# The seams of a three-stage sequence kernel: the first norm of its last block and its stores moved into the streams, keys and first maxima merged with the groups before them, and four heads scored at once where no maxima are due

## The chip, the cores and the metric

The kernel runs on one core of one Trainium2 chip. The metric is the time of one execution on the device in microseconds (us), and lower is better. Data are float32, with a few masks and index vectors in bfloat16.

Engines: PE does matmuls (PEld is its load of weights, which overlaps), DVE vector operations, ACT activations and copies, POOL further vector operations, and SP issues most DMAs. Each engine takes its own queue in order. PE writes into PSUM, which here is eight banks of 128 partitions x 512 floats; DVE and ACT read the results from there.

## The reference, cut to what matters

One sequence `x` of 2048 tokens with 128 features passes through four residual blocks:

```python
x = x + L0_attn(layernorm(x))   # LinOSS state space model, gated
x = x + L0_ffn(layernorm(x))    # 8 experts, top 1: relu(h @ We[e] + be[e]) * p
x = x + L1_attn(layernorm(x))   # causal attention, 16 heads of 8, softmax
x = x + L1_ffn(layernorm(x))    # 6 layers, each: local attention (16 heads of 64,
                                # windows of 32, rotary), then a gated feed-forward
```

The state space model is a recurrence along time, `z1 = m11 z + m12 y + f1 bu`, `y1 = m21 z + m22 y + f2 bu`, with two components (real and imaginary) for each of 128 states; then `o = ys[0] @ C0.T - ys[1] @ C1.T + x * D`, normed, multiplied by a gate `g * sigmoid(g)` and projected. The causal attention needs, for each query and head, the maximum of its scores (or any value that keeps the exponentials in range), the exponentials, their sum and the weighted values. The last block is itself a small network whose input is `layernorm(x)`; its output is added to `x`.

## The kernel before

**Grid.** 2048 tokens are 16 tiles of 128 (NT), and 4 groups (NG) of 4 tiles, each group 512 tokens wide (GW). Almost every operation on PSUM is 128 x 512.

**Order of work.** The wrapper `InOrder` (line 59) keeps what it issues in program order on its engine, so the order in which the Python code calls `self.pe`, `self.dve` and so on is the order of the queues. The trace names the wrapper's line, 66, for all of these; they are told apart by the names of their tiles. `interleave` (line 71) merges generators: each job yields how long to wait in a made-up time, and the one that is due first goes on.

**Stages 1 and 2 (`front`, line 458).** `ssm_inputs` (line 244) of each group, started 5.0 apart: layer norm (`norm_transposed`), `px` into `xsT`, two `pb` into `f1`, then `pg`, the gate. `ssm_scan` (line 277) then runs on DVE: 16 steps inside chunks of 16 tokens, a doubling scan over the 128 chunks, and 16 steps that give `yo`, one operation for each component. POOL meanwhile forms the powers (`ssm_powers`) after it has finished the gates. Then a second `interleave` (line 513) merges, for each group, `ssm_out`, `experts` and `keys_values`. An expert group holds two banks, `pi` and `py`, while DVE makes eight masked copies `own` (8 buffers) and PE multiplies each with its expert's matrix. `keys_values` makes the normed input `hT3`, the values `va`, and the keys `kT` for four groups of four heads. The PSUM pool of this part has 8 banks.

**Stage 3 (`stages123`, line 521).** The causal attention, for 16 blocks: 4 groups of heads times 4 groups of queries. Two streams of units:

- `maxima` (line 570): for one tile of queries and up to 512 keys, scores of two heads, then of the other two (`part`), then DVE's `reduce_max` (`rest`). When a block's maxima are done, `finish` subtracts them from the queries (`qT`), and only then may the block's attention begin.
- `attend` (line 627): for one tile of keys, scores of two heads at a time, `exp` on ACT, POOL's causal mask on the diagonal, and `pieces`, the weighing of the values (`av` on PE), put off by two half units.

Four heads' matmuls take 32 rows of the array each. The loop at line 758 runs ahead with the maxima: some units alone (the `while` at line 761), most paired with an attention unit (two heads of each at once), and where the maxima are far enough ahead an attention unit goes without them, still as two halves of two heads. `pass_unit` runs steps that were put off: `back`, `out_a`, `out_b`, which turn a finished block's result, project it, add `x` and write `x3T` (line 722). The pool of stage 3 has 7 banks under one tag and one for `av`.

**Stage 4 (`stage4`, line 807).** It first loads tables (`rot`, 1 MB, line 820) and masks, and norms `x3T` group by group into `s4[0]` (lines 853 to 861, with `norm_columns`, line 1192): mean by a matmul, difference, square, mean by a matmul, power on POOL, spread by a matmul, product. Then 96 tile steps (6 layers x 16 tiles) run as one software pipeline (`steps`, line 1172), in which `feed_forward` (line 1164) gives each step its parts of a group's feed-forward. Each tile also issues 14 to 16 small DMAs (`vw`) on SP. At the end `store` (line 1217) adds `x3T`, turns the result and stores it group by group: `yT`, `pst`, `ot`.

## Time and profile before

| | us |
|---|---|
| median of three runs (2693.87 to 2695.86) | 2695.79 |
| the profiled execution | 2700.82 |
| its span, first to last instruction | 2699.1 |
| SSM inputs, until the scan's first operation | 0 to 44.3 |
| scan on DVE, PE idle | 44.3 to 100.1 |
| SSM output, experts, keys and values | 100.1 to 207 |
| first maxima; first attention scores at 220.7 | 207 to 222 |
| attention, until the last `x3T` | 222 to 878 |
| first norm of stage 4, until its first projection | 878 to 909.5 |
| stage 4, with the stores at its end | 909.5 to 2699.1 |

Busy over the whole span: PE 2459.0 us (91%), DVE 1821.7 (67%), POOL 1658.8 (61%), ACT 1349.7 (50%). The mean granted clock of PE was 0.971.

How to read it: a timeline row gives start, duration, engine, line, operation, output and inputs, shapes, count, and, in brackets, the idle time of the engine before it with what ended it. A float32 matmul shows as two rows (`x2` for one). A row with a count covers that many instructions. A wait for several semaphores is put down to the last by the profile.

### The profile page before, as it was taken

To read this page: it belongs to the slowest core of one execution; us is meant where nothing else is said; L and a number is where in the kernel's file an instruction comes from. 1 tells how busy PE (TensorE), PEld (TensorE's weight loads), DVE (VectorE), ACT (ScalarE), POOL (GpSimd) and SP (SyncE) were. 2 spreads that over 40 slices of the span, in tenths; PEclk is the share of its full clock that TensorE was granted. 3 is DMA by queue.
4 is the path that set the end of the run, shared out by engine and by line. 5 is a ranking of instruction groups with operands and counts; after the bars stand their busy time and mean duration, and the time that the engine had idled before them with its cause. 6 is when DMAs were issued, how large, how long until landed. Compare 5 with 4: busy or idle time off the path is not lost.

```text
span 2699.1 us, 85362 instructions
## 1 busy us (share of the span) xinstructions
PE 2459.0 (91%) x37600; PEld 1478.4 (55%) x37600; DVE 1821.7 (67%) x2764; ACT 1349.7 (50%) x1806; POOL 1658.8 (61%) x1011
## 2 busy tenths in 40 slices
PE   3489999999999689999999999999999999999997
PEld 1473333333333366666666666666666666666664
DVE  6766664476642467777777777777777777777774
ACT  1132455544555144555555555555555555556552
POOL 4310000000001599989888888898888988898980
PEclk8689999999999799999999999999999999999999
DMA  2000000000000222233222322232323222222221
GB/s 82 1 1 1 1 1 1 2 1 1 1 1 1 62 65 69 60 88 72 59 66 67 89 58 71 66 87 60 73 62 82 69 66 67 59 60 65 60 59 43
DMA packets 93566, 128.39 MB, mean 48 GB/s; under 512 B 26248, under 2 KB 41104, under 8 KB 93072
## 3 DMA queue, kind: packets, MB, share of 16 engines
q1 hardware_dynamic: 92620, 122.48, 18.6%
q8 instruction: 299, 4.90, 0.8%
q10 hardware_dynamic: 580, 0.46, 0.1%
q14 instruction: 67, 0.55, 0.1%
HBM read 20.35 MB, written 1.05 MB: 8 GB/s over the span
## 4 chain that ended last, share of the span: by engine, by line
PE 63%; DVE 21%; ACT 6%; issue 5%; POOL 4%; SPq 1%; DMA 0%; DVEq 0%; ACTq 0%; POOLq 0%
PE sc L66 17%; PE ps L66 10%; PE av L66 6%; PE pt L66 5%; DVE mx L66 4%; PE py L66 4%; DVE rot_a L66 4%; DVE sm L66 4%; DVE ss L66 4%; PE ph L66 3%; DVE rot_b L66 3%; PE pto L66 3%; PE ptp L66 3%; ACT sq L66 3%; POOL sm L66 2%
## 5 line engine op out<-in xcount | busy, mean ns | idle before, releaser
L66 DVE TENSOR_REDUCE mx<-sc 128x1 f32<-128x512 f32 (+4 forms) x736 | 471.0, 685 | 238.9 <-PE sc L66 234.1
L66 POOL TENSOR_TENSOR rot_a<-rot_a,rot_b 128x1024 f32<-128x1024 f32 x192 | 459.2, 2392 | 144.1 <-DVE rot_b L66 143.9
L66 POOL TENSOR_TENSOR rn<-ss,mhalf 128x32 f32<-128x32 f32 x96 | 523.9, 5457 | 8.0
L66 ACT ACTIVATE ex<-sc 128x512 f32<-128x512 f32 (+3 forms) x640 | 310.0, 531 | 302.4 <-PE sc L66 301.3
L66 PE MATMUL sc<-kT,qT 64*32 64x64 f32 (+2 forms) x13568 | 429.7, 260 | 9.6 <-ACT qT L66 9.3
L66 POOL TENSOR_SCALAR_AFFINE_SELECT ex<-ex 128x512 f32<-128x512 f32 x64 | 40.6, 634 | 628.2 <-ACT ex L66 628.2
L66 DVE TENSOR_TENSOR rot_a<-ps,tab 128x1024 f32<-128x1024 f32 x192 | 235.0, 1224 | 221.9 <-ACT sq L66 205.3
L66 PE MATMUL sc<-qT,kT 32*128 32x512 f32 (+3 forms) x1280 | 369.4, 581 | 2.3 <-DVE qT L66 2.1
L66 PE MATMUL ps<-wqkv,s 128*128 128x512 f32 x768 | 367.8, 602 | 1.5 <-DVE rd L66 1.5
L66 ACT COPY vt<-pv 128x1024 f32<-128x1024 f32 x96 | 97.2, 1013 | 443.4 <-PE pv L66 425.4
L66 PEld LDWEIGHTS sc<-kT,qT 64*32 64x32 f32 (+1 forms) x13568 | 221.5, 113 | 139.1 <-issue 68.9
L66 ACT ACTIVATE sq<-ps 128x1024 f32<-128x1024 f32 x192 | 195.9, 1020 | 101.4 <-PE ps L66 101.4
L66 DVE TENSOR_REDUCE ss<-sq 128x16 f32<-128x1024 f32 x192 | 233.1, 1214 | 2.8
L66 DVE TENSOR_TENSOR rot_b<-ps,tab 128x1024 f32<-128x1024 f32 x192 | 233.0, 1213 | 0.0
L66 PEld LDWEIGHTS pt<-ident,rot_a 128*128 128x128 f32 x1536 | 175.5, 142 | 76.8 <-issue 40.3
L66 PEld LDWEIGHTS px<-oT,wo 128*128 128x128 f32 x1536 | 182.3, 193 | 63.5 <-ACT oT L66 61.4
L66 PEld LDWEIGHTS ps<-wqkv,s 128*128 128x128 f32 x768 | 138.6, 191 | 141.5 <-issue 136.7
L66 ACT ACTIVATE ex<-sm 128x1024 f32<-128x1024 f32 x96 | 101.5, 1057 | 221.2 <-POOL sm L66 221.2
L66 PE MATMUL pt<-ident,rot_a 128*128 128x128 f32 x1536 | 188.3, 275 | 23.3 <-POOL rot_a L66 23.1
L66 POOL TENSOR_TENSOR sm<-sm,rn 128x1024 f32<-128x1024 f32 x96 | 183.5, 1911 | 40.6 <-DVE rd L66 18.7
L66 DVE SCALAR_TENSOR_TENSOR act<-ph,vec,ge 128x512 f32<-128x512 f32 (+1 forms) x72 | 54.0, 750 | 220.1 <-ACT ge L66 220.0
L66 PE MATMUL px<-oT,wo 128*128 128x128 f32 x1536 | 194.9, 280 | 6.7 <-ACT oT L66 6.7
(212 smaller groups left out, 4014.2 us busy)
## 6 DMA issues: line engine op xcount, KB each, us to landing
vw<-vt SPq DMA_DIRECT2D x1524, 65.0 KB, 2.0
wqkv<-in_L_ffn_Wqkv SPq DMA_DIRECT2D x18, 512.0 KB, 5.1
wo<-in_L_ffn_Wo SPq DMA_DIRECT2D x6, 512.0 KB, 4.7
w<-in_L_ffn_W SPq DMA_DIRECT2D x6, 341.0 KB, 3.3
x<-in_L_attn_hidden_states SPq DMA_DIRECT2D x4, 256.0 KB, 4.3
rot<-in_rot SPq DMA_DIRECT2D x1, 1024.0 KB
out<-ot SPq DMA_DIRECT2D x4, 256.0 KB, 2.2
w<-in_L_ffn_W SPq DMA_DIRECT2D x12, 64.0 KB, 2.6
```

The lines of the kernel that those rows point to most:

```text
L66: return self._tc.keep_in_program_order(call(*args, **kw))
```

## The change

It has five parts, quoted below with lines left out where marked.

- `Merge` takes the place of `interleave`: jobs may be added while it runs, and it can stop when named jobs are done.
- SSM inputs: groups start 2.5 apart, the gate's projection waits 14.0 instead of 4.0; the two components of `yo` are written by one operation, into the memory of `f1`; the gate lies in the memory of `x3T`.
- `keys_values` makes the keys of the first head group alone; `keys` makes the others as a job of its own. The first maxima start as a job at 76, among the experts, and the attention is a job that is merged with what is left. The early part shares the 7 banks of the attention; `own` has 4 buffers.
- An attention unit without maxima scores all four heads, then weighs.
- The first norm of stage 4 is three put-off steps behind `out_b`; the stores are an eighth part of `feed_forward`, `yT` being formed in the last `ff_down` of a group. `rot` is loaded in two pieces.

```diff
+class Merge:
+    def __init__(self):
+        self.due, self.n, self.now = [], 0, 0.0
+    def add(self, wait, job):
+        heapq.heappush(self.due, (self.now + wait, self.n, job))
+        self.n += 1
+        return job
+    def run(self, jobs=None):
+        left = None if jobs is None else set(map(id, jobs))
+        while self.due and left != set():
+            self.now, _, job = heapq.heappop(self.due)
+            wait = next(job, None)
+            if wait is not None:
+                self.add(wait, job)
+            elif left is not None:
+                left.discard(id(job))
...
         self.dve.tensor_copy(xs_g, px)
-        yield 2.0
+        yield 3.0
...
-        yield 4.0
+        yield 14.0
         pg = psum.tile([P, G, P], F32, name="pg", tag="b")
...
-            for c in range(2):
-                dve.scalar_tensor_tensor(
-                    yo[c].rearrange("p (k l) -> p k l", l=CL)[:, :, l], cy[:, c], rows[:, 1, l : l + 1], t[:, c],
-                    ALU.mult, ALU.add,
-                )
+            dve.scalar_tensor_tensor(
+                yo.rearrange("p c (k l) -> p c k l", l=CL)[:, :, :, l], cy, rows[:, 1, l : l + 1], t,
+                ALU.mult, ALU.add,
+            )
...
-            own = pool.tile([P, GW], F32, name="own", bufs=EXPERTS)
+            own = pool.tile([P, GW], F32, name="own", bufs=4)
...
-        for grp in range(NGRP):
+        yield from self.keys(psum, g, hT3, kT, [0])
+
+    def keys(self, psum, g, hT3, kT, grps):
+        wqk, bqk, wv, wo, bo = self.w3
+        hg = hT3[:, g * GW : (g + 1) * GW]
+        for grp in grps:
             pk = psum.tile([P, GW], F32, name="pk", tag="b")
...
-            psum = ctx.enter_context(tc.tile_pool(name="s1p", bufs=8, space=PSUM))
...
-            begin = [(0, 9, 43), (9, 22, 58), (7, 40, 77), (18, 57, 82)]
...
+        begin = [(0, 9, 43, 51), (10, 22, 58, 66), (7, 41, 74, 87), (16, 57, 91, 111)]
+        wait = []
+        for g, (a, b, c, d) in enumerate(begin):
+            wait.append(merge.add(a, self.ssm_out(pool, psum, x, g, gate, xsT, yo)))
+            wait.append(merge.add(b, self.experts(pool, psum, x, g)))
+            merge.add(c, self.keys_values(kvpool, psum, x, g, hT3, kT, va))
+            merge.add(d, self.keys(psum, g, hT3, kT, range(1, NGRP)))
+        return wait
...
                     act.activation(xT[:, g * GW : (g + 1) * GW], po, AF.Identity, bias=bo)
+                    later(1, lambda: norm_a(g))
...
+            def norm_a(g):
+                xg = xT[:, g * GW : (g + 1) * GW]
+                pm = bank("pm")
+                pe.matmul(pm, lhsT=self.mean_w, rhs=xg, start=True, stop=True)
+                xc = pool.tile([P, GW], F32, name="nxc", tag="av", bufs=3)
+                dve.tensor_tensor(xc, xg, pm, ALU.subtract)
+                sq = pool.tile([P, GW], F32, name="nsq", tag="av", bufs=3)
+                act.activation(sq, xc, AF.Square)
+                later(1, lambda: norm_b(g, xc, sq))
+            def norm_b(g, xc, sq):
+                pvar = bank("pvar")[:, 0:G]
+                for j in range(G):
+                    pe.matmul(
+                        pvar[:, j : j + 1], lhsT=sq[:, j * P : (j + 1) * P], rhs=self.mean_w[:, 0:1],
+                        start=True, stop=True,
+                    )
...
+                self.rsqrt(r, var)
+                later(1, lambda: norm_c(g, xc, r))
+            def norm_c(g, xc, r):
+                pr = bank("prb")
...
+                    dve.tensor_tensor(
+                        self.s4_in[rs, g * GW + h : (g + 1) * GW + h], xc[rs], pr[rs], ALU.mult
+                    )
...
+            def catch_up(b, c):
+                nonlocal ahead
+                while ahead is not None and done - ahead[1] < wanted(b, c) - GW:
                     for rest in [step_m(ahead, pr) for pr in range(2)]:
                         rest()
                     pass_unit()
                     ahead = next_m()
-                while b not in found:
+                    yield 1.6
+            def weigh_due():
+                if pieces and pieces[0][0] <= halves:
+                    pieces.pop(0)[1]()
...
+                    if ahead is not None and done - ahead[1] < wanted(b, c_now):
+                        for half in range(2):
+                            rest = step_m(ahead, half)
+                            part(1 - half)
+                            weigh_due()
+                            if half:
+                                whole()
+                            rest()
+                            halves += 1
+                        pass_unit()
+                        ahead = next_m()
+                    else:
+                        for half in range(2):
+                            part(1 - half)
+                        weigh_due()
+                        halves += 1
+                        weigh_due()
+                        whole()
+                        halves += 1
+                        pass_unit()
+                    c_now += wd
+                    yield 3.3 * wd / GW
...
+            def begin():
+                nonlocal ahead
+                ahead = next_m()
+                yield 1.5
+                yield from catch_up(0, 0)
+            ahead = None
+            lead = merge.add(76.0, begin())
+            merge.run(wait)
+            early.close()
...
+            merge.run([lead])
+            merge.add(0.0, attention())
+            merge.run()
...
-            nc.sync.dma_start(rot, a["rot"])
+            for i0, i1 in ((0, 1), (1, NT)):
+                nc.sync.dma_start(rot[:, i0:i1], a["rot"][:, i0:i1])
...
-            for g in range(NG):
-                cols = slice(g * GW, (g + 1) * GW)
-                xc = pool.tile([P, GW], F32, name="xc")
-                pr = self.norm_columns(xc, x3T[:, cols], mean_w, pool, psum)
...
+                if g // NG == DEPTH - 1:
+                    yT = ff[g]["y"] = pool.tile([P, GW], F32, name="yT", tag="xc")
...
+                        dve.tensor_tensor(yT[rs], s4[0][rs, n + h : n + h + GW], x3T[rs, n : n + GW], ALU.add)
...
+            def store(g):
+                if g // NG == DEPTH - 1:
+                    yT = ff[g].pop("y")
+                    pt = big("pst")[:, 0].rearrange("p (j c) -> p j c", c=P)
+                    for j in range(G):
+                        pe.transpose(pt[:, j, :], yT[:, j * P : (j + 1) * P], self.ident)
+                    ot = pool.tile([P, G, P], F32, name="ot", tag="ff")
+                    dve.tensor_copy(ot, pt)
+                    sp.dma_start(o[:, g % NG * G : (g % NG + 1) * G, :], ot)
             parts = [
-                ff_mean, ff_var, ff_norm, lambda g: ff_up(g, 0), lambda g: ff_up(g, 1), lambda g: ff_up(g, 2), ff_down
+                ff_mean, ff_var, ff_norm, lambda g: ff_up(g, 0), lambda g: ff_up(g, 1), lambda g: ff_up(g, 2),
+                ff_down, store,
             ]
...
-            self.store(s4[0], x3T, out, pool, psum)
```

## The prediction, made before the result was known

> **What bounds the kernel now.** I read the table of 40 slices first, then the timeline at each place where PE falls off. In the slices (67.5 us each) PE is at nine tenths nearly everywhere; the exceptions are slices 1 to 3, slice 14 and the last, and in all but the last the granted clock falls as well.

> ```profile
> PE   3489999999999689999999999999999999999997
> ...
> DVE  6766664476642467777777777777777777777774
> ...
> PEclk8689999999999799999999999999999999999999
> ...
> PE 63%; DVE 21%; ACT 6%; issue 5%; POOL 4%; SPq 1%; DMA 0%; DVEq 0%; ACTq 0%; POOLq 0%
> ```

> The last line, the chain that ended last, says the same: PE 63%, with DVE as the second. So PE time counts wherever PE is full (the attention and stage 4), and waiting counts at the seams. The busy times of the stretches, from the query by windows (the columns after the length: PE, PEld, DVE, ACT, POOL, then clock, DMA share, GB/s), size the seams:

> ```profile
> 0.00:44.20 44.20, 25.34 (x72) 12.76 (x72) 18.85 (x68) 11.15 (x17) 7.27 (x13) 1.00 0.43 125
> 44.20:100.10 55.90, 0.00 (x0) 0.00 (x0) 52.91 (x123) 1.02 (x3) 39.76 (x93) 0.54 0.00 0
> ...
> 193.80:222.00 28.20, 21.55 (x111) 10.13 (x111) 14.56 (x40) 7.93 (x13) 3.92 (x6) 1.00 0.00 1
> 222.00:232.00 10.00, 10.00 (x45) 4.99 (x44) 5.53 (x15) 2.24 (x4) 0.64 (x1) 0.52 0.00 0
> ...
> 878.00:909.50 31.50, 19.79 (x73) 13.94 (x74) 7.74 (x17) 2.52 (x4) 6.46 (x17) 0.66 0.38 122
> ```

> The first is the SSM's inputs, with no engine full; the second the scan, which is DVE alone; the third the seam into the attention; the fourth the half clock behind it; the fifth the first norm of stage 4, one chain of waits per group.

> **Part a, the SSM inputs.** In the timeline the scan's first DVE operation starts at 44.28. DVE starts at 7.5 and owes each group 1.8 us of statistics (four pairs at 0.40, one 0.17), 1.1 of normalising, 0.69 for xsT and 1.07 for f1: 4.66, so 18.6 for four. The other 18 us it waits for PE (px 2.07 and pb 3.78 at low clock, 1.13 and 1.98 at full) in an order that lets a group's gate stand between. The change starts groups 2.5 apart, not 5, and moves the gates behind all f1. Following the new order with these durations, each DVE step waiting for the PE step before it, I get xsT of groups 0 and 1 at 16.5 and 21.6, then 5 us a group: f1 of group 3 ends at 36.7 (clock up early) to 38.5. I take **-6.5**; bounds -3 and -9. The gates (PE, ACT, POOL 1.27 each) go under the scan. POOL's powers are queued behind them: they ran from 47.3 to 71.6 and were needed at 82.7, so with the scan 6.5 earlier and the gates ending near 43 about 7 us of slack remain.

> **Part b, the scan.** Each of 16 steps now has one update of 128x256 where two of 128x128 stood (two in 0.54, start to start). Two independent 128x256 ones take 0.40 each (the zt pairs at 71.9 to 82.7), so 16 x 0.14 = **-2.2**.

> **Part c, keys and first maxima inside the early groups.** From 193.8 to 222 PE does 21.6 us of work; 6.6 us are idle: the last group's norm waits for the experts' sum, then pq for the keys, maxima for q, and DVE's last three reductions for the subtraction that frees the first scores. The next 10 us run at clock 0.52, a loss of 4.8. Within 100.1 to 193.8 PE is busy 83.2 of 93.7, another 10.5 of gaps. Nothing is removed; keys of groups 1 to 3 and the last two groups' values move into the attention's opening, where PE waits for maxima. Filled entirely, 6.6 + 4.8 + about half of 10.5 = 16.6. Against it: 4 own buffers where DVE ran 8 ahead (at 180.7, eight in 4.86 us, while PE takes 1.28 for each; queued behind the waiting fifth own is only the next group's statistics, whose transposes PE reached 4 us later anyway), and 7 banks for 8. I take **-11**, bounds -4 and -17. [...] The longest PE gap before the half clock is 2.14 us (218.6 to 220.74)[...]. The row shows the fall right behind the gaps, and I go by the row.

> **Part d, four heads at once.** When no maxima are due, a unit scored two heads, weighed, scored two, weighed:

> ```profile
> 838.56 1.13 PE L66 MATMUL sc<-qT,kT 32*128 32x512 f32 x4
> ...
> 839.61 0.64 PE L66 MATMUL av<-ex,va 128*32 128x256 f32 x8
> ...
> 840.18 1.13 PE L66 MATMUL sc<-qT,kT 32*128 32x512 f32 x4
> ...
> 841.24 0.64 PE L66 MATMUL av<-ex,va 128*32 128x256 f32 x8
> ...
> 515.18 1.14 PE L66 MATMUL sc<-qT,kT 32*128 32x512 f32 x8
> ```

> The first four rows are one such unit, 838.56 to 841.81: 3.25. The last is a place where nothing was ready to weigh: four heads (x8) in the 1.14 that two took, since each uses its own 32 rows. The new order makes every such unit 1.07 + 2 x 0.57 = 2.21. Running the loop of line 758 by hand over the widths (160 score units, 160 maxima units) leaves 40 attention units without maxima, 3 of them already joined: 26 of width 512 save 1.05 each, 4 of 384 0.84, 2 of 256 0.63, 5 of 128 0.42; in all 34.1. Eight stand behind catch-up maxima, where PE waits for DVE: half lost, -4; the narrow ones, and the last 12 in a row, wait for exponentials and POOL's mask: -5. So **-25**. [...] ACT's row for four exponentials is 2.06 (at 837.54), under the 2.21, so they fit if they lie beside the next weighing. [...]with scores and emptying in turn, a unit costs 1.07 + 2.06 = 3.13, and the part is 37 x 0.12 = -4.5. Bounds -4.5 and -34.

> **Part e, the first norm.** Group 0's chain ran from 878.3 to 887.3 (pm, subtraction 0.69, square 0.63, pvar 1.55, POOL power 1.01, prb 2.08, two products 1.39). What stage 4 needs first is just this, yet its first projection stood in PE's queue behind the other groups:

> ```profile
> 877.30 0.69 ACT L66 ACTIVATE x3T<-po,bo 128x512 f32<-128x512 f32 x1 [3.42 <-PE po L66]
> ...
> 883.76 2.08 PE L1211 MATMUL prb<-ident,fr 128*128 128x128 f32 x8 [1.35 <-POOL fr L66]
> ...
> 885.88 1.39 DVE L859 TENSOR_TENSOR s<-xc,prb 64x512 f32<-64x512 f32 x2 [3.26 <-PE prb L1211]
> ...
> 909.48 8.27 PE L66 MATMUL ps<-wqkv,s 128*128 128x512 f32 x16
> ```

> Moving groups 3, 2 and 1 into the attention gives 909.5 - 887.3 = 22.2. They still cost PE 0.9 + 1.0 + 0.9 each at full clock: 8.7 in all. Group 3's is fully paid. Group 1's prb, in program order ahead of group 0's po, waits for POOL's power, and the last chain behind it loses about 2.6. The idle 3.7 us of 833 to 878 cover a little. So **-14**, bounds -12 and -20. POOL's masks then queue behind a 1.01 power. The rot load was issued at 878.04, 31 us ahead; now it is late next. Its first 64 KB go alone (65 KB land in 2.0 by the issue table), tab takes 0.73, and rot_a stood 4.3 behind the first projection: it fits; if not, +2 inside the bounds. The load of 960 KB behind it is needed 9 us in, carry 26.

> **Part f, the stores.** After the last py (2689.4) come the update of s (1.53), then a copy and an addition of other groups before the last group's own addition, transposes and copy, ending 2695.85:

> ```profile
> 2689.48 1.53 DVE L66 SCALAR_TENSOR_TENSOR s<-py,vec,s 64x512 f32<-64x512 f32 x2
> 2691.04 0.69 DVE L1231 COPY ot<-pst 128x512 f32<-128x512 f32 x1
> 2691.77 2.12 DVE L1224 TENSOR_TENSOR yT<-s,x3T 64x512 f32<-64x512 f32 x3
> ...
> 2695.16 0.69 DVE L1231 COPY ot<-pst 128x512 f32<-128x512 f32 x1 [0.55 <-PE pst L1229]
> ```

> With the others gone: 2691.0 + 1.4 + 0.7 + 0.8 = 2693.9, 1.9 less, and two additions that held up act by 0.7 each save perhaps 0.6: **-2.5**, bounds -1 and -4. Three of the four 256 KB stores now enter SP's queue behind a tile's vw loads and wait there for ot; the vw loads behind each belong to the next step and aren't ready before it. Without that cover a store's wait of some 2 us would be paid three times.

> **The sum.** -6.5 - 2.2 - 11 - 25 - 14 - 2.5 = -61.2. The profiled execution took 2700.8 (span 2699.1 and 1.7 around it), so it becomes 2639.6; it stands 5.0 above the median of the runs, 2695.8, so the median becomes **2634.6**, ratio 0.977. Stage 4's order inside the streams is the same, some 1760 us that I leave alone.

> **The rivals.** First, the emptying of PSUM sets the pace (d is -4.5): -40.7, **2655**. For it: 7 banks, and four are taken at once; against it, ACT is busy only 25.9 of 45 at 833 to 878. Second, the cover is better than I allow (a -9, b -2.2, c -17, d -32, e -19, f -4): -83, **2613**; for it, the 34.1 and 22.2 are read directly, and the gaps are many. Third, merging gives nothing (c at 0), since DVE's maxima set the pace of the opening either way (DVE is busy 75.1 of 108 at 222 to 330, with PE waiting for mx 22.6 us between 205 and 420): **2646**. Fourth, on the other side: the shared banks. All early work, maxima too, draws on 7 where 8 served it, and py and pi keep theirs through an expert group of 12 us. PE takes its queue in order, so one allocation without a free bank stops everything. Some 52 allocations lie between the scan and the attention; if each waits 1.2 us more, the 61 are eaten, and beyond that the change is **slower**: at 2 us each, 104 - 61 = +43, 2739. Against it: with 8 banks the waits that look like this there (py, pv, pl on ACT) sum to 1.2 us.

> **How the numbers follow.** My forecast 0.56; better cover 0.13; PSUM 0.14; no gain from merging 0.12; banks 0.03; and 0.02 that the parts cancel to nothing. What a measurement of this kernel can tell is about 0.2%, 5.4 us. Faster 0.95, same 0.02, slower 0.03. My own range, parts at moderate ends, is 2618 to 2652. To leave out no more than 2 in 10 it takes in the third rival and reaches towards the first and the second: **2612 to 2658**.

> **What would show it.** Right: the scan's first operation near 38; first score of the attention proper near 200, without a slice at half clock; in the tail sc<-qT,kT x8 in about 1.14, units of 2.2 to 2.5; no L1211 chain, the first ps within 12 us of the last x3T; one yT pair and one ot behind the last py. Wrong: PE waiting for ACT ex at every such unit; PE waiting in the early groups for releases; the first ps late behind rot or the masks; stage 4's spacing, 18 us a tile, changed.

## The result and the profile after

The changed kernel takes 2655.45 us (median of four runs, 2653.21 to 2659.93) against 2695.82: ratio 0.9852, 95% interval 0.9835 to 0.9869. It is faster by 40.4 us. The forecast was 2634.6, 61.2 less, with a range of 2612 to 2658. The direction held, the time lies 2.5 inside the range's slow end, and a third of the expected gain did not come. The first rival, in which the emptying of PSUM sets the pace, had 2655, the measured time almost to the digit; the run on part d below tells whether it was right. The profiled execution took 2653.21, with a span of 2651.5; as that of before lay 5.0 above its median and this one 2.2 below, the two profiles differ by 47.6.

First the table of 40 slices of the changed kernel, and its chain that ended last:

```profile
PE   3589999999998689999999999999999999999997
...
DVE  7775765476652577777777777777777777777774
...
PEclk8797999999999899999999999999999999999999
...
PE 60%; DVE 23%; ACT 6%; issue 6%; POOL 5%; DMA 0%; SPq 0%; DVEq 0%; POOLq 0%; ACTq 0%
```

The low slices are still 1 to 3, those at the seam to stage 4 (the 13th to 15th) and the last. The fourth slice (199 to 265), where the keys and the first maxima now lie among attention units, has PE at nine tenths but the clock at 0.7. The query by windows shows where (columns after the length: PE, PEld, DVE, ACT, POOL, then clock, DMA share, GB/s). The rows are the SSM inputs, the scan, the stretch ahead of the first attention score, two stretches behind it, and the last `x3T` to the first projection of stage 4:

```profile
0.00:36.41 36.41, 20.59 (x53) 9.58 (x54) 18.73 (x69) 8.70 (x11) 5.06 (x13) 1.00 0.50 152
36.41:93.04 56.63, 2.32 (x22) 2.16 (x21) 53.97 (x107) 3.69 (x8) 44.66 (x99) 0.56 0.00 0
187.00:200.00 13.00, 10.08 (x75) 4.95 (x73) 11.10 (x26) 2.15 (x6) 1.26 (x1) 1.00 0.00 1
200.00:207.00 7.00, 7.00 (x19) 2.54 (x20) 1.14 (x5) 2.59 (x5) 0.65 (x1) 0.51 0.01 2
217.00:231.00 14.00, 12.45 (x52) 5.55 (x50) 7.97 (x17) 1.46 (x3) 0.64 (x1) 0.51 0.00 0
853.00:862.78 9.78, 4.25 (x18) 3.08 (x19) 2.79 (x8) 1.31 (x2) 4.19 (x15) 0.80 0.71 244
```

The inputs end 7.9 earlier, the scan is not shorter (55.9 before), the seam to stage 4 (from the start of the last `x3T` to that of the first projection) has shrunk from 32.2 to 9.8, and behind the first attention score, 20.9 earlier than before, stand two stretches at half clock.

Cut at points that both kernels have, with the prediction's parts beside it, the two profiles differ so. Blocks count from 1, a block's end is the start of its ACT copy `avs`, the scan's end is the first `po` on PE, and `ps` is stage 4's projection.

| stretch | before | after | difference | forecast |
|---|---|---|---|---|
| start to the scan's end (a, b) | 100.14 | 93.04 | -7.1 | -8.7 |
| to the end of the third block (c, 1 of d) | 250.39 | 250.99 | +0.6 | -12 |
| to the first `ps` (the rest of d, e) | 558.95 | 518.75 | -40.2 | -38 |
| to the end (f) | 1789.6 | 1788.7 | -0.9 | -2.5 |
| sum | 2699.1 | 2651.5 | -47.6 | -61.2 |

So the missing part lies in one row above all, the second. The timeline of PE in the changed kernel shows the parts that worked, the four heads at once and the short norm of group 0:

```profile
816.83 1.14 PE L66 MATMUL sc<-qT,kT 32*128 32x512 f32 x8
817.90 1.07 PE L66 MATMUL av<-ex,va 128*32 128x256 f32 x16
818.90 0.66 PE L66 MATMUL pto<-ident,ao 128*128 128x128 f32 x4
819.49 1.14 PE L66 MATMUL sc<-qT,kT 32*128 32x512 f32 x8
820.56 1.07 PE L66 MATMUL av<-ex,va 128*32 128x256 f32 x16
...
853.73 1.13 PE L66 MATMUL pm<-x3T,mean_w 128*128 128x512 f32 x2 [0.78 <-ACT x3T L66]
856.36 1.05 PE L66 MATMUL pvar<-mean_w,nsq 128*128 128x1 f32 x8 [1.50 <-ACT nsq L66]
859.18 2.08 PE L66 MATMUL prb<-ident,nr 128*128 128x128 f32 x8 [1.77 <-POOL nr L66]
862.78 7.73 PE L66 MATMUL ps<-wqkv,s 128*128 128x512 f32 x14 [1.52 <-issue]
```

A unit of four heads, scores and weighing, is 2.07 from start to start of the next operation (816.83 to 818.90), where it was 3.25.

### The profile page after: what moved, and what is told of

Same layout as the page of the kernel before. It is cut to its first block, busy times and chain, and to the rows that moved or that the text cites. A ratio compares the mean times of both kernels' runs of the same rounds, so it can differ in the third digit from the quotient of the medians.

```text
span 2651.5 us, 85346 instructions
## 1 busy us (share of the span) xinstructions
PE 2420.8 (91%) x37600; PEld 1466.8 (55%) x37600; DVE 1823.7 (69%) x2746; ACT 1345.0 (51%) x1806; POOL 1658.9 (63%) x1013
## 3 DMA queue, kind: packets, MB, share of 16 engines
HBM read 20.35 MB, written 1.05 MB: 8 GB/s over the span
## 4 chain that ended last, share of the span: by engine, by line
PE 60%; DVE 23%; ACT 6%; issue 6%; POOL 5%; DMA 0%; SPq 0%; DVEq 0%; POOLq 0%; ACTq 0%
PE sc L66 16%; PE ps L66 10%; PE av L66 6%; PE pt L66 5%; DVE mx L66 4%; DVE rot_a L66 4%; DVE ss L66 4%; DVE sm L66 4%; DVE rot_b L66 3%; PE ptp L66 3%; PE pto L66 3%; PE ph L66 3%; ACT sq L66 3%; PE py L66 3%; POOL sm L66 2%
## 5 line engine op out<-in xcount | busy, mean ns | idle before, releaser
L66 DVE TENSOR_REDUCE mx<-sc 128x1 f32<-128x512 f32 (+4 forms) x736 | 471.0, 685 | 230.4 <-PE sc L66 226.1
L66 POOL TENSOR_TENSOR rot_a<-rot_a,rot_b 128x1024 f32<-128x1024 f32 x192 | 457.0, 2380 | 152.3 <-DVE rot_b L66 149.5
L66 POOL TENSOR_TENSOR rn<-ss,mhalf 128x32 f32<-128x32 f32 x96 | 524.0, 5458 | 8.0
L66 ACT ACTIVATE ex<-sc 128x512 f32<-128x512 f32 (+3 forms) x640 | 306.0, 536 | 278.8 <-PE sc L66 277.9
L66 PE MATMUL sc<-kT,qT 64*32 64x64 f32 (+2 forms) x13568 | 426.3, 259 | 8.4 <-ACT qT L66 7.8
L66 POOL TENSOR_SCALAR_AFFINE_SELECT ex<-ex 128x512 f32<-128x512 f32 x64 | 40.8, 637 | 578.2 <-ACT ex L66 562.1
L66 DVE TENSOR_TENSOR rot_a<-ps,tab 128x1024 f32<-128x1024 f32 x192 | 235.1, 1224 | 221.0 <-ACT sq L66 209.1
L66 PE MATMUL ps<-wqkv,s 128*128 128x512 f32 x768 | 368.5, 603 | 3.6 <-DVE rd L66 2.1
L66 PE MATMUL sc<-qT,kT 32*128 32x512 f32 (+3 forms) x1280 | 340.5, 583 | 4.0 <-DVE qT L66 2.1
L66 ACT COPY vt<-pv 128x1024 f32<-128x1024 f32 x96 | 97.3, 1013 | 441.2 <-PE pv L66 423.1
L66 PEld LDWEIGHTS sc<-kT,qT 64*32 64x32 f32 (+1 forms) x13568 | 219.9, 112 | 138.2 <-issue 71.9
L66 ACT ACTIVATE sq<-ps 128x1024 f32<-128x1024 f32 x192 | 196.0, 1021 | 102.1 <-PE ps L66 102.1
L66 DVE TENSOR_REDUCE ss<-sq 128x16 f32<-128x1024 f32 x192 | 233.0, 1214 | 2.8
L66 DVE TENSOR_TENSOR rot_b<-ps,tab 128x1024 f32<-128x1024 f32 x192 | 233.0, 1214 | 0.0
L66 PEld LDWEIGHTS pt<-ident,rot_a 128*128 128x128 f32 x1536 | 175.5, 142 | 80.4 <-issue 42.4
L66 PEld LDWEIGHTS ps<-wqkv,s 128*128 128x128 f32 x768 | 138.7, 191 | 143.7 <-issue 138.5
L66 PEld LDWEIGHTS px<-oT,wo 128*128 128x128 f32 x1536 | 182.0, 193 | 63.4 <-ACT oT L66 61.4
L66 ACT ACTIVATE ex<-sm 128x1024 f32<-128x1024 f32 x96 | 101.5, 1057 | 222.4 <-POOL sm L66 222.4
L66 PE MATMUL pt<-ident,rot_a 128*128 128x128 f32 x1536 | 188.7, 275 | 26.4 <-POOL rot_a L66 24.3
L66 DVE SCALAR_TENSOR_TENSOR act<-ph,vec,ge 128x512 f32<-128x512 f32 (+1 forms) x72 | 53.9, 749 | 226.2 <-ACT ge L66 226.2
L66 POOL TENSOR_TENSOR sm<-sm,rn 128x1024 f32<-128x1024 f32 x96 | 183.6, 1913 | 38.7 <-DVE rd L66 18.6
L66 PE MATMUL px<-oT,wo 128*128 128x128 f32 x1536 | 195.1, 281 | 6.2 <-ACT oT L66 6.2
```

The costliest lines, as they stand in the source:

```text
L66: return self._tc.keep_in_program_order(call(*args, **kw))
```

## The experiments

Each run is the changed kernel with one edit, unless said otherwise. Times differ a little from chip to chip (the kernel before had 2693.09 to 2698.76 on the five used below), so each is given as its ratio to the kernel before on the same chip. The changed kernel itself was run twice more beside them.

> The changed kernel itself, as the base for the runs beside it on this chip: ratio to the kernel before 0.985, interval of 0.0017 either side.

> The changed kernel as the base on this chip: ratio to the kernel before 0.985, interval of 0.002 either side.

They gave 0.9848 (0.9828 to 0.9869) and 0.9852 (0.9830 to 0.9873); with the first, 0.9851 on average. One thousandth is 2.7 us.

### Part d undone

```diff
-                        for half in range(2):
-                            part(1 - half)
-                        weigh_due()
-                        halves += 1
-                        weigh_due()
-                        whole()
-                        halves += 1
+                        for half in range(2):
+                            part(1 - half)
+                            weigh_due()
+                            if half:
+                                whole()
+                            halves += 1
```

> The changed kernel with part d alone undone: units without maxima score two heads, weigh, score two, weigh again. Forecast of the prediction (d worth 25): 2655 + 25 = 2680. The rival in which the emptying of PSUM sets the pace (d worth 4.5): 2660. The reading of the trace after (a unit takes 2.07 where it took 3.25, and blocks 2 to 15 of the attention are 22 shorter although three norm groups were added): 2680 to 2686. In the trace sc<-qT,kT x4 at 1.13 each should stand again in the last two blocks.

2679.94, ratio 0.9942 (0.9920 to 0.9964): 24.6 slower than the changed kernel. In the profiles, third block to last block is 26.7 longer (527.6 against 500.8), against the 24 that the forecast has there. The emptying of PSUM as the pace (4.5) is out: that its sum, 2655, was met is chance, since it took from part d what in truth was missing from part c and others. ACT's row shows that exponentials and weighing do lie beside each other; this is ACT in the changed kernel, at the units shown above:

```profile
818.05 2.07 ACT L66 ACTIVATE ex<-sc 128x512 f32<-128x512 f32 x4 [0.46 <-PE sc L66]
819.98 0.62 ACT L66 COPY aoT<-pto 128x512 f32<-128x512 f32 x1
820.71 2.06 ACT L66 ACTIVATE ex<-sc 128x512 f32<-128x512 f32 x4
```

### Part c undone

```diff
-        yield from self.keys(psum, g, hT3, kT, [0])
+        yield from self.keys(psum, g, hT3, kT, range(NGRP))
...
-        begin = [(0, 9, 43, 51), (10, 22, 58, 66), (7, 41, 74, 87), (16, 57, 91, 111)]
+        begin = [(0, 9, 43), (9, 22, 58), (7, 40, 77), (18, 57, 82)]
...
-            lead = merge.add(76.0, begin())
             merge.run(wait)
...
-            merge.run([lead])
+            lead = merge.add(0.0, begin())
+            merge.run([lead])
```

(`wait` holds the jobs of `keys_values` too, and `keys` is no job of its own.)

> The changed kernel with part c alone undone: all keys of a group directly behind its values, the first maxima only behind all early groups, start times as in the kernel before. Forecast of the prediction (c worth 11): 2655 + 11 = 2666. Rival, merging gives nothing because the waits and the half clock only move: 2655, within 3. In the trace the half-clock stretches decide: if merging had helped, the time from the scan's end to the end of the third block's weighing (250.4 before, 251.0 after) should be about 11 longer here; by the rival it is the same.

2661.11, ratio 0.9859 (0.9835 to 0.9882): 2 slower than the changed kernel, with an interval of some 6 either side. In time alone a part of the 11 could hide, so the profile has to decide. The run keeps the 7 banks and the 4 `own` buffers, so it tests the order of the work alone. From the scan's end to the end of the third block, one window for each kernel, first the kernel before, then the changed one, then this one:

```profile
100.14:350.53 250.39, 230.21 (x1586) 131.40 (x1588) 164.22 (x405) 85.23 (x217) 26.46 (x32) 0.91 0.00 1
```

```profile
93.04:344.03 250.99, 231.33 (x1588) 130.88 (x1590) 165.06 (x404) 84.92 (x216) 24.93 (x28) 0.90 0.00 1
```

```profile
92.08:343.17 251.09, 230.43 (x1588) 130.53 (x1590) 164.75 (x404) 84.67 (x216) 24.87 (x28) 0.90 0.00 1
```

The number of matmuls is the same within 2, PE's busy time within 1.1, the clock within 0.01, and the length within 0.7. PE is idle for 20.2, 19.7 and 20.7: the merge filled almost none of it. How far such a stretch scatters is seen in the nine profiles that keep the changed kernel's order there (its own three, and those of part d undone, which differs in its last units alone, of part e undone, of part f undone twice, of the third version of f, and of the gates on DVE): 246.8 to 251.1. So nothing of part c's 11 is seen, as in the third rival; a gain of 2 would not show.

### What the waits cost: keys in the gap

PE of the changed kernel, around its first attention score:

```profile
197.20 0.49 PE L66 MATMUL sc<-kT,qT 32*128 32x128 f32 x4
199.83 1.77 PE L66 MATMUL sc<-qT,kT 32*128 32x512 f32 x4 [2.14 <-DVE qT L66]
...
204.53 3.17 PE L66 MATMUL pk<-hT,wqk 128*128 128x512 f32 x4
...
215.24 0.91 PE L66 MATMUL sc<-qT,kT 32*128 32x384 f32 x2 [1.69 <-DVE mx L66]
...
221.40 0.90 PE L66 MATMUL ln_pt<-ident,ln_h 128*128 128x128 f32 x3 [1.55 <-DVE ln_h L66]
```

The 2.14 for `qT` is the one of the kernel before, where the row was

```profile
220.74 1.13 PE L66 MATMUL sc<-qT,kT 32*128 32x512 f32 x4 [2.14 <-DVE qT L66]
```

It is still there, and the keys that could fill it stand behind it in PE's queue, where they run at half clock (0.51 from 200 to 207). The run puts them ahead, by running that generator (`self.fill`) there and not as a job:

```diff
+                    for _ in self.fill:
+                        pass
                     if ahead is not None and done - ahead[1] < wanted(b, c_now):
```

> The changed kernel with the three remaining key projections of group 2 (1.07 each at full clock) placed in PE's 2.14 wait ahead of the first attention score, instead of behind the first unit. Theory of the prediction (the half clock falls because of that gap): no half clock from 200 to 207, so 2.1 of wait and some 3 of half clock go, and the time from the scan's end to the end of the third block's weighing becomes about 5 shorter than 251. Rival ([...]merging only moves waits): the half-clock stretches stay or come elsewhere, that time stays within 2 of 251, and the kernel stays within 3 of the changed one.

From the scan's end to the third block's end it took 246.70, 4.3 less than the changed kernel's profile. Its window from 200 to 207 and its row at the keys:

```profile
200.00:207.00 7.00, 6.66 (x43) 3.22 (x40) 4.30 (x12) 2.54 (x5) 0.64 (x1) 1.00 0.01 2
```

```profile
196.82 2.74 PE L66 MATMUL pk<-hT,wqk 128*128 128x512 f32 x6
...
199.54 0.70 PE L66 MATMUL sc<-qT,kT 32*128 32x512 f32 x2
```

The wait for `qT` is gone, and with it the half clock in this place (0.51 in the changed kernel). The next half clock starts at 212.3, behind the wait for DVE `mx`, which this run left in, and a third runs from 243.0 to 256.7. Over the whole stretch PE is idle for 17.5, where the nine profiles have 18.7 to 19.7: the wait itself was won. The half clock was not: it lasts 48.2 in all, within the 41.5 to 52.7 of the nine, and so 246.70 lies at the edge of their lengths. Here the rival, that the half clock moves, fits the sum, and the theory fits the place. The time, 2653.40, ratio 0.9838 (0.9818 to 0.9858), is 2.9 below that of the changed kernel beside it, too little for its interval.

### The gates under the scan

DVE of the changed kernel at the start of the scan, then POOL's work there:

```profile
36.80 0.48 DVE L66 SCALAR_TENSOR_TENSOR zt<-kT,pw 128x256 f32<-128x256 f32 x1
37.24 5.49 POOL L66 TENSOR_TENSOR x3T<-x3T,sg 128x512 f32<-128x512 f32 x4 [17.18 <-ACT x3T L66]
37.31 1.48 DVE L66 SCALAR_TENSOR_TENSOR zn<-kT,pw,zt 128x256 f32<-128x256 f32 x1
...
40.23 1.37 DVE L66 SCALAR_TENSOR_TENSOR zt<-kT,pw 128x256 f32<-128x256 f32 x1
...
43.04 0.48 DVE L66 SCALAR_TENSOR_TENSOR kT<-zn,dt,kT 128x256 f32<-128x256 f32 x1
```

Four steps take 1.37 to 1.48 in place of 0.48, just while POOL makes its four products of 1.37. In the kernel before, two of the gates ran beside the scan and two DVE steps were long; now all four do. The run gives `sg` memory of its own (that of `s4`), so that it lasts until the product is made:

```diff
-        self.gps.tensor_tensor(gg, gg, sg, ALU.mult)       # ssm_inputs
...
+        self.dve.tensor_tensor(gg, gg, self.sg[:, g * G : (g + 1) * G, :], ALU.mult)   # ssm_out, behind po
```

> The changed kernel with POOL's four gate multiplications (1.37 each, beside the scan's first steps) given to DVE, one at the head of each group's output step behind the scan. Theory: POOL's 512-wide multiplications hold DVE up, which is why four DVE steps of the scan take 1.37 to 1.48 instead of 0.48; then the scan shortens from 56.6 to about 53, DVE pays 4 x 0.69 later, the first under po, and the kernel is about 2 to 3 faster than the changed one. Rival (the prediction's own assumption): the gates are free under the scan and the long steps have another cause; then the scan stays at 56.6 and the kernel is the same or up to 2.8 slower.

The scan took 52.4 instead of 56.6 to 56.7; at its start no step was longer than 0.77. The run moves more than the gates: POOL, no longer held by the gates, formed the powers ahead of the scan (from 20 on, not from 43) and its other small tables early in it. So of the 4.3 only 2.9 lie in the first 45 steps, beside the gates; 1.3 lie in the doubling steps, of which two pairs had taken 1.42 in place of 0.87 beside POOL's tables. Behind the scan nothing is seen to be lost (246.9 to the third block's end). The first `ps` came 6.5 earlier than in the changed kernel beside it, but in the times this is 2653.26 against 2656.30, ratios 0.9847 (0.9823 to 0.9872) and 0.9848: not to be told apart. That POOL's products hold up DVE's steps is shown by the two profiles: one step of 1.37 to 1.48 for each product, and none over 0.77 there without them. By what means they do, and a gain in time, are not shown.

### Part e undone

```diff
-                    later(1, lambda: norm_a(g))
...
+            for g in range(NG):                            # in stage 4, as before
+                xc = pool.tile([P, GW], F32, name="xc")
+                pr = self.norm_columns(xc, x3T[:, cols], mean_w, pool, psum)
```

> The changed kernel with part e alone undone: stage 4 again begins with the norm of all four groups. Forecast of the prediction (22.2 gained less 8.7 of PE time for three groups moved in): 2655 + 14 = 2669. Rival, the moved groups are hidden in waits of the attention's end and cost nothing: 2655 + 22 = 2677. Rival, what is gained at the seam is lost in a later start of stage 4's first tiles (rot, masks): 2655 to 2660.

2668.70, ratio 0.9896 (0.9880 to 0.9912): 12.2 slower than the changed kernel, against the forecast's 14; the two rivals, 22 and 0 to 5, are out. In the profile the last block's end to the first `ps` is 37.95 (17.9 to 20.4 in the changed kernel's three), and the last three blocks are 5.4 shorter without the groups.

### Part f undone, and moved

```diff
-                ff_down, store,
+                ff_down,
...
+            self.store(s4[0], x3T, out, pool, psum)        # behind the loop, as before
```

> The changed kernel with part f alone undone: the four last additions, transposes, copies and stores stand behind all streams again. Forecast of the prediction (f worth 2.5): 2658. Reading of the trace after: the end behind the last update is 1.9 shorter, but the stretch before it is 1.9 longer, with PE held 1.44 for yT of group 2; by that the part is worth 0 to 1: 2655 to 2656, and here the interval from first ps to the last update of s should be about 1779 instead of 1781.

> Once more the changed kernel with the stores behind all streams, beside the changed kernel on the same chip, since two executions of the same stage 4 lie up to 8 apart. If the stores in the streams cost more than they save: 3 to 6 faster than the changed kernel. If the part is worth nothing either way: within 2. If the prediction's 2.5 holds: 2.5 slower.

2651.02, ratio 0.9828 (0.9813 to 0.9843), and 2650.26, ratio 0.9840 (0.9815 to 0.9865), with the changed kernel at 0.9852 beside the latter. On average this is 4.5 faster than the changed kernel, with intervals that overlap, so the times alone do not settle it. The distances between the last updates of `s` say more: but for the first, they are the same to 0.1 within each kind of kernel, as is the rest behind the last one.

| | third from last | second from last | last | to the end |
|---|---|---|---|---|
| before | 68.3 | 14.9 | 8.8 | 9.6 |
| changed kernel, three profiles | 66.4 to 69.4 | 16.8 | 9.9 | 7.8 |
| stores last, two profiles | 64.4, 65.0 | 14.9 | 8.8 | 9.6, 9.7 |

The 1.9 forecast behind the last update did come, and 1.9 + 1.1 went just ahead of it: a loss of 1.1 is shown, the rest of the 4.5 is not. PE and DVE in the changed kernel:

```profile
2635.41 1.40 DVE L66 TENSOR_TENSOR yT<-s,x3T 64x512 f32<-64x512 f32 x2
...
2636.95 0.63 PE L66 MATMUL pst<-ident,yT 128*128 128x128 f32 x4 [1.44 <-DVE yT L66]
2637.42 3.60 PE L66 MATMUL ph<-xc,w 128*128 128x512 f32 x8
```

PE waits for group 2's sum with the last group's `ph` behind it in the queue. With the stores last (below, that kernel at the same place) the `ph` run through in 5.39 and the transposes come later, where PE waits anyway:

```profile
2630.78 5.39 PE L66 MATMUL ph<-xc,w 128*128 128x512 f32 x12
```

A third version put each addition one step ahead of its transposes, in the last group's own steps:

```diff
+            drain = {
+                0: [(total, end - 3)], 1: [(store, end - 3), (total, end - 2)], 2: [(store, end - 2)],
+                4: [(total, end - 1)], 5: [(store, end - 1)], 6: [(total, end)], 7: [(store, end)],
+            }
```

> The changed kernel with the stores of groups 0 to 2 of the last layer moved into the last feed-forward group's own steps, each addition one step ahead of its transposes; only the last group's stay behind its update. Theory (the changed kernel's stores stand in PE's and DVE's full streams and cost there what they save at the end): from first ps to the end it is 1778.1 + 7.8 = 1786 instead of 1788.7 (changed) and 1787.7 (all stores last), so about 2.5 faster than the changed kernel. Rival (the difference of 2.9 in that stretch is scatter between executions): within 1.5 of the changed kernel.

2652.99, ratio 0.9842 (0.9823 to 0.9861): the four distances are 64.3, 18.0, 10.2 and 7.8. Its second and third distances are 4.5 longer than with the stores last, for 1.9 less at the end, and its 1787.5 from first `ps` to end is no better than theirs (1787.7, 1785.8).

### What the runs point to, together

The joined kernel has the gates on DVE, group 2's keys in the gap, the stores last, and two edits against PE's other waits: five `own` buffers, and the norm of group 3 started where DVE stood idle.

```diff
-            own = pool.tile([P, GW], F32, name="own", bufs=4)
+            own = pool.tile([P, GW], F32, name="own", bufs=5)
...
-        begin = [(0, 9, 43, 51), (10, 22, 58, 66), (7, 41, 74, 87), (16, 57, 91, 111)]
+        begin = [(0, 9, 43, 51), (10, 22, 58, 66), (7, 41, 74, 87), (16, 57, 86, 111)]
```

> The changed kernel with what the runs so far point to: gates on DVE behind the scan, group 2's keys in the 2.14 wait, the stores behind all streams, five own buffers, and group 3's norm started right behind the first attention unit (start 86 instead of 91), where DVE stood idle, so that its statistics no longer hold the maxima (PE waited 1.69 for DVE mx) nor ln_h the transposes (1.55). If PE's short waits bring the half clock, the stretch at half clock behind them (some 14 us of PE from 217 to 231) goes too: from the scan's end to the end of the third block's weighing about 237 instead of 251, and the kernel some 15 to 20 faster than the changed one, 2636 to 2641. If the half clock comes whatever the waits: about 245 there, and 2646.

2632.32, ratio 0.9769 (0.9748 to 0.9789), against 0.9852 (0.9830 to 0.9873) for the changed kernel on the same chip: 22 faster than it, and 61 faster than the kernel before. From the scan's end to the third block's end:

```profile
89.81:326.54 236.73, 218.81 (x1588) 124.46 (x1590) 166.96 (x408) 85.11 (x216) 25.96 (x28) 0.94 0.00 1
```

This is 14.3 less than in the changed kernel's first profile, and 10.1 to 14.4 less than in the nine, with the same 1588 matmuls. Against the first, PE is idle 17.9 instead of 19.7; the other 12.5 is that the same matmuls take less time, at a clock of 0.94 (half clock lasts 30.0 in all, not 52.5). Which of the five edits brought that was not tested one by one: alone, the gates, the keys and the stores measured some 3 to 4.5 each, and none clear of noise. One wait of 4.09 was new (from 196.85, `ln_h` of group 3, in front of ready scores), with half clock from 198.4 to 208.6. The last run takes that one away, by starting the norm at 87 and letting its transposes come later:

```diff
+        if gap is not None:        # 2.0 for group 3's keys, between ln_h and its transposes
+            yield gap
```

> The joined kernel with one wait less: in it PE waited 4.09 for ln_h of group 3 (196.9 to 200.9), and its clock was half from 200 to 207. Here that group's norm starts at 87 instead of 86 and its transposes come 2.0 later than its ln_h, so two units of scores for maxima stand in PE's queue where the wait was. If the half clock follows PE's waits: no stretch at half clock near 200, and from the scan's end to the end of the third block's weighing about 231 instead of 236.7 (some 2 to 3 of the wait, some 3 of half clock), the kernel near 2627. If the half clock comes by itself: 234, the kernel near 2630, with a half-clock stretch still between 195 and 215. If DVE's maxima set the pace there in any case (seven banks): PE waits for DVE mx instead, 236 to 237 and no gain.

The stretch fell to 232.21, near the 231 of the first theory, with a clock of 0.96:

```profile
89.11:321.32 232.21, 216.91 (x1588) 124.12 (x1590) 165.93 (x408) 84.76 (x217) 26.05 (x28) 0.96 0.00 1
```

But not in its way. PE now waits for DVE `mx` in that place, the third theory's wait:

```profile
197.44 0.69 PE L66 MATMUL sc<-kT,qT 32*128 32x256 f32 x2 [1.62 <-DVE mx L66]
```

A half clock from 200.6 to 207.4 still follows it, and it is the later stretch, 246 to 253 in the joined kernel, that is gone, without a known cause. The time, 2638.26 (2626.07 to 2643.97), ratio 0.9777 (0.9751 to 0.9803), doesn't differ from the joined kernel's.

## Why the prediction was right, and where not

- **Part a** (-6.5): the scan started 7.9 earlier (36.41; 35.5 to 37.3 in all runs). "The gates go under the scan" at no cost was wrong: two more DVE steps are stretched by 0.9 each, since POOL's products run just beside them.
- **Part b** (-2.2): 0.9, of which 0.5 is a wait in the old row. The merged operation was costed at 0.40 from start to start, read from pairs of independent operations. Here each step needs the one before, and it takes 0.50 where the pair took 0.54. It also writes every 16th element and is recorded as 0.65 long; which of the two counts was not tested. Scan and inputs together: -7.1 for -8.7.
- **Part c** (-11): this is the step that failed, by its whole size. Its sum put the wait (6.6), the half clock (4.8) and half of the earlier gaps (10.5) to the order of the work, to be filled by merging. But the waits belong to chains (maxima, turned maxima, subtraction, first score; statistics, power, `ln_h`), and PE took its queue in order: the merge moved both chains and left almost the same waits, 2.14 to the hundredth, and the keys that could fill one ran behind it (204.53, the score at 199.83). The third rival said this ("c at 0") and gave it 0.12. Its reason was that DVE's maxima set the pace. The 22.6 that it read as PE's waits for `mx` are waits of the weight loads (PEld); PE itself has none for `mx` there. For the 2.14 the run shows the order instead: moving three key projections a few places up the queue took it away. Elsewhere the maxima do hold PE (1.69 here, 1.62 in the last run).
- **The clock** inside part c was read rightly from the row and wrongly used. In the changed kernel the half clock stayed, behind waits of 2.14 and 1.69, and where the 2.14 was filled it did not come in that place (1.00 from 200 to 207, against 0.51). So the row was right that half clock followed that wait. The error was to take for granted that the waits, and all of the half clock with them, would vanish.
- **Part d** (-25): 24.6 by time. The full-width units read take 2.07, where 2.21 was forecast, and "PE waiting for ACT ex at every such unit" did not come. (The savings listed add to 34.0, not 34.1.)
- **Part e** (-14): 12.2 by time. The terms as written (22.2, 8.7, 2.6) leave 10.9, and 14.6 if all of the idle 3.7 is cover, so the -14 took nearly all of it; the result lies between. `prb` of group 1 did wait for POOL (0.92) ahead of group 0's `po`; first `ps` 9.8 behind the last `x3T`; the rot load was in time.
- **Part f** (-2.5): wrong in sign. The end behind the last update was right to the tenth (1.9), but "the vw loads behind each belong to the next step" watched only SP's queue; the cost came on PE's and DVE's, 3.0 in the last two groups. The version without the part is some 4.5 faster in intervals that overlap.
- **The shared banks**: the rival on the slow side named 52 allocations. Between the scan and 232, PE waits for a bank once in the changed kernel (1.69, DVE `mx`). With 4 `own` buffers there are four waits for `own`, 1.5 in all, where there had been one of 0.27.

By times the parts are -7.1 (a, b, from the profile), 0 to -2, -24.6, -12.2 and +1.1 to +4.5: -39 to -45, for the measured -40.4. The time was in the range because d and e, two thirds of the forecast, were read from single rows and came, and because the range had been widened to take in the third rival, c at 0.

## What to carry to other kernels

A gap in an engine that takes its queue in order is filled only if something ready stands ahead of the waiting instruction in that queue (three key projections moved ahead of the first score took away the 2.14); merging jobs by start times moves a gap as easily as it fills it, so list, for each wait, what is to stand in its place. Work "under" another engine's work may cost that engine time, as POOL's products did DVE (steps of 1.37 for 0.48), and work put into a full stream is paid there (3.0 for the stores). What counts around such waits can be less the wait than the clock: 12.5 of the 14.3 between the profiles of the changed and the joined kernel are matmuls that ran at a higher clock. And a stretch whose clock shifts from execution to execution is to be judged by several profiles, not by one.

## What the runs showed of the hardware

```profile
196.79:200.20 3.41, 1.27 (x10) 0.84 (x11) 2.99 (x5) 0.00 (x0) 0.00 (x0) 1.00 0.01 2
200.20:203.61 3.41, 3.41 (x14) 1.10 (x10) 0.49 (x2) 1.08 (x2) 0.00 (x0) 0.50 0.00 0
```

- With all 14 traces cut on their grids from 104 to 400, a window at full clock in which PE was busy for less than 60% was followed by half clock in 34 of 38 cases; at 60 to 75% in 17 of 54, and above in 21 of 957. In these counts the fall goes with PE's share of a window: the 2.14 (from 197.69) fell into one window and was followed by half clock from 200.2 to 207.0, with PE busy throughout. The same order of work got more or less half clock from execution to execution (41.5 to 52.7 in the nine profiles above). Of the 21, some come behind windows in which PE was never idle (248.0 to 261.6 in the changed kernel); what brings those was not found.
- DVE beside POOL: in the changed kernel, 128x512 products on POOL (1.37 each) stretched DVE's 128x256 steps from 0.48 to 1.37 one for one, while POOL's products of 128 x 1 to 128 x 2 behind them left the steps at 0.48. POOL's small products took longer themselves beside the scan: a pair of 128 x 8 took 0.83 there (at 66.56), and 0.36 where it ran ahead of the scan (at 33.95, in the run with the gates on DVE).
- Profiles of the same stage 4 differ by up to 5.3 from first `ps` to end (1788.7, 1791.0, 1794.0 in the changed kernel), so a part worth 3 us there must be read from the distances that repeat, not from the sum.
